# Scatters of the edges' records in small groups beside the nodes' tiles, each group behind one product of its tile

## The chip, the core and the metric

The kernel runs on one core of a Trainium2 chip. A core has TensorE (PE, matrix products; its weight loads are shown as PEld), VectorE (DVE), ScalarE (ACT), GpSimd (POOL) and SyncE (SP), each with a queue of its own that is worked off in order. They signal each other through semaphores. DMA engines move data; here SP and ACT issue the plain transfers, POOL the indirect ones (gathers and scatters by an index list) and some plain ones. The metric is the device time of one execution in microseconds.

## What is computed

A graph layer over 3125 nodes with 512 features and 50000 edges sorted by target node, then a mixture of experts. Cut to what matters:

```python
xn = _layernorm(x)
x = x + gnn(xn, edge_attr_4, edge_attr_32, [src, dst], ...) + mix(xn, ...)   # mix: linear attention over all nodes
x = x + moe(_layernorm(x), ...)

# gnn, for each edge: a gather of both ends' rows, products, and a sum at one end
edge_dst, edge_src = edge_index[0], edge_index[1]
ip1 = einsum('eum,eum->eu', p1[edge_dst], p1[edge_src]) / 3
w = ssp(edge_attr @ W_f1) @ W_f2 * (ssp(s0 @ W_s1) @ W_s2)
out = segment_sum(edge_feat(w, x[edge_src], edge_sh), edge_dst)

# mix: k' and the sums over all nodes first, then every node's query against them
kv = einsum('bshd,bshf->bhdf', k_prime, v)
z = einsum('bshd,bhdf->bshf', q_prime, kv) / (q_prime . k_prime.sum + 1e-6)
```

## The kernel before, in words

The edges are put in order on the chip. There are T = 392 tiles of 128 edges, in 14 chunks of CT = 28 tiles, and NT = 25 tiles of 128 nodes.

*Sort and layer norms.* `records(c)` computes for chunk c, on VectorE, the place of each edge in the sorted list (`places`, into `at_i`) and makes for each edge a record of 48 numbers (its four spherical numbers, both node numbers, the hidden row of its 32 attributes). The chunk's records go to a DRAM tensor `lined` (L262). Between the chunks, the loop at L366 runs `layer_norm(t)` for one or two node tiles: mean and variance, a normalised tile `xn`, four transposes on TensorE (L345), a copy of them by ScalarE into `xT` (L346), the product with the key weights `ps_k` (L349), the feature map (VectorE L303, ScalarE L304, VectorE L305), and two products `ps_kx` (L353) that add this tile to sums over all nodes. So each tile passes from engine to engine some ten times; buffers of two tiles let neighbours overlap.

*Scatters.* POOL takes the records of a chunk back into SBUF (`recall`, L399, two buffers `again`) and scatters them, one indirect DMA of 128 records for each of the 392 edge tiles (L407), to their sorted places in `recs`. It needs a chunk's `lined` and its `at_i`, and nothing else. In the program the loop stands behind all the layer norms; as POOL's queue holds nothing else there, it runs as soon as its data are there.

*Folding, queries, nodes' tiles.* The sums are folded with value and output weights into `kvw` and `norm` (L463 to L500). The queries (L507 on) run over 7 chunks of 512 nodes and 2 groups of heads: products `ps_q`, feature map, one product `ps_nm` (L518) and a division. Then, for each chunk of 512 nodes, the gate network, and for each node tile t the rows that the edges will gather, `rows_d` and `rows_s` (L592, L593), and the node's own part: `ps_own` gets two products of the query (L598) and four of the gated features (L602), and is added to `out` (L606). Four PSUM buffers serve `ps_p1` and `ps_nd`, two serve `ps_own`, so PE can be about two tiles ahead of those who empty them.

*Edge loop.* The first load of sorted records (`fetch`, q = 0) waits for all 392 scatters. Then POOL gathers the two ends' rows for each tile of edges (L658, L662), which also need `rows_d` and `rows_s` complete. The loop over 220 pairs of edge tiles runs in an order written out by hand. The mixture of experts follows.

The order on each engine is made by a scheduler from the order of the program and the dependencies; `tc.issue_after` holds an instruction behind another in that order.

Of the kernel before, what the change touches and what calls it, by code (L numbers as in the profile page):

```python
# [8 lines left out]
F32 = mybir.dt.float32  # L9
# [7 lines left out]
P = 128  # L17
# [4 lines left out]
REC = 48  # L22
USED = 40
CT = 28
# [14 lines left out]
def gnn_mix_moe_kernel(ctx: ExitStack, tc: tile.TileContext, a: dict, out: bass.AP):  # L39
# [5 lines left out]
    nc = tc.nc  # L45
    N = a["x"].shape[0]
    T = a["src_t"].shape[1]
# [36 lines left out]
    lined = dram.tile([T // CT, P, CT, REC], F32, name="lined")  # L84
    recs = dram.tile([NQ * G * P, REC], F32, name="recs")
# [12 lines left out]
    def waits_for(ins, other):  # L98
        tc.add_manual_dep(
            ins.ins, other.ins.name,  # L100
            mybir.DependencyInfo(mybir.DependencyClass.Sync, mybir.DependencyReason.DATA),
            reason="rows at places known on the chip alone",
        )
# [11 lines left out]
    with ExitStack() as c1:  # L115
        srt = c1.enter_context(tc.tile_pool(name="srt", bufs=1))
        chk = c1.enter_context(tc.tile_pool(name="chk", bufs=2))
# [20 lines left out]
        for r in range(4):  # L138
# [10 lines left out]
        cleared = [  # L149
            nc.gpsimd.dma_start(  # L150
                flat[k * P * zw : (k + 1) * P * zw].rearrange("(p f) -> p f", p=P), zero
            )
            for k in range(10)
        ]
# [42 lines left out]
        at_i = srt.tile([P, T], I32, name="at_i")  # L197
# [26 lines left out]
        placed = []  # L224
# [91 lines left out]
        def layer_norm(t):  # L316
            nonlocal fresh
            n = tn(t)
            rows = slice(t * P, t * P + n)
            x = lnp.tile([P, D], F32, name="x")  # L320
            with tc.issue_after(lines[-2].ins):
                nc.sync.dma_start(x[:n], a["x"][rows, :])
            st = lnp.tile([P, 6], F32, name="bn")
            with tc.issue_after(found[-2].ins):
                nc.vector.bn_stats(st[:n], x[:n])
            mv = lnp.tile([P, 2], F32, name="mv")
            nc.vector.bn_aggr(mv[:n], st[:n])

            rs = lnp.tile([P, 1], F32, name="rs")
            nc.scalar.activation(rs[:n], mv[:n, 1:2], AF.Ln, bias=eps[:n])  # L330
            fresh = nc.scalar.activation(rs[:n], rs[:n], AF.Exp, scale=-0.5)
            off = lnp.tile([P, 1], F32, name="off")
            nc.vector.scalar_tensor_tensor(off[:n], mv[:n, 0:1], -1.0, rs[:n], op0=ALU.mult, op1=ALU.mult)
            rs1 = lnp.tile([P, 1], F32, name="rs1")
            nc.vector.tensor_single_scalar(rs1[:n], rs[:n], 1.0, op=ALU.add)
            xn = lnw.tile([P, D], F32, name="xn")
            nc.scalar.activation(xn[:n], x[:n], AF.Identity, scale=rs[:n], bias=off[:n])

            y = lnw.tile([P, D], F32, name="so_far")
            nc.scalar.activation(y[:n], x[:n], AF.Identity, scale=rs1[:n], bias=off[:n])  # L340
            nc.vector.tensor_add(y[:n], y[:n], b_add[:n])
            nc.sync.dma_start(out[rows, :], y[:n])
            ps = psum.tile([P, 4, P], F32, name="ps_t", tag="mm")
            for b in range(4):
                nc.tensor.transpose(ps[:, b, :n], xn[:n, b * P : (b + 1) * P], ident[:n, :n])  # L345
            nc.scalar.copy(xT[:, :, rows], ps[:, :, :n])  # L346
            ps_k = psum.tile([P, NH * FD], F32, name="ps_k", tag="mm")
            for k in range(4):
                nc.tensor.matmul(ps_k[:n], xT[:, k, rows], w_rk[:, k, :], start=(k == 0), stop=(k == 3))  # L349
            kf = lnw.tile([P, NH * FD], F32, name="kf")  # L350
            feature_map(kf[:n], ps_k[:n], n, NH * FD, lnw, NH * FD)
            for g in range(2):
                nc.tensor.matmul(  # L353
                    ps_kx[g], kf[:n, g * P : (g + 1) * P], xn[:n], start=(t == 0), stop=(t == NT - 1)
                )
            nc.vector.tensor_add(kfs[:n], kfs[:n], kf[:n])

        with tc.issue_after(found[0].ins):
            nc.vector.tensor_add(b_add[:, :MUL], b_add[:, :MUL], b_o0)
# [3 lines left out]
        ps_b = psum.tile([P, P], F32, name="ps_bo", tag="mm")  # L363
        nc.tensor.matmul(ps_b, b_row, w_o[0], start=True, stop=True)
        nc.vector.tensor_add(b_add[:, :MUL], b_add[:, :MUL], ps_b)
        for c in range(1, NC):  # L366
            records(c)
            for t in range((c - 1) * NT // (NC - 1), c * NT // (NC - 1)):
                layer_norm(t)
            if c == 3:  # L370
                with tc.issue_after(fresh.ins):
                    w_g1 = load("w_g1", [P, 2, 2 * MUL], a["W_g1"].rearrange("(k p) f -> p k f", p=P))
                    w_g2 = load("w_g2", [P, 2, 2 * MUL], a["W_g2"].rearrange("(k p) f -> p k f", p=P))
                    b_g1 = load("b_g1", [P, 2], a["b_g1"])
                    b_g2 = load("b_g2", [P, 2], a["b_g2"])
                    w_pre0 = load("w_pre0", [P, MUL], a["W_pre0"])
                    b_pre0 = load("b_pre0", [P, 1], a["b_pre0"])
                    w_pre1 = load("w_pre1", [P, MUL], a["W_pre1"])
                    w_nd0 = load("w_nd0", [P, MUL], a["W_nd0"])
                    w_nd1 = load("w_nd1", [P, MUL], a["W_nd1"])  # L380
                    b_nd0 = load("b_nd0", [P, MUL], _rows(a["b_nd0"], P, MUL))
                    w_s1 = load("w_s1", [P, 2, HID], a["W_s1"][0 : 2 * MUL, :].rearrange("(k p) f -> p k f", p=P))
                    w_v = load("w_v", [P, 4, D], a["W_v"].rearrange("(k p) f -> p k f", p=P))
                    w_out = load("w_out", [P, 4, D], a["W_out"].rearrange("(k p) f -> p k f", p=P))
            elif c == 5:
                with tc.issue_after(fresh.ins):
                    w_rq = by_random("W_qT")
# [2 lines left out]
        with tc.issue_after(made.ins):  # L390
            nc.vector.tensor_add(w_s1p, w_s1[:, 0, :], w_s1[:, 1, :])


        again = {}

        def recall(c):
            if c < T // CT:
                again[c] = chk.tile([P, CT, REC], F32, name="again", bufs=2)
                nc.gpsimd.dma_start(again[c], lined[c])  # L399

        recall(0)
        for c in range(T // CT):
            for i in range(CT):
                t = c * CT + i
                if i == CT // 2:
                    recall(c + 1)
                put = nc.gpsimd.indirect_dma_start(  # L407
                    out=recs[:, :], out_offset=bass.IndirectOffsetOnAxis(ap=at_i[:, t : t + 1], axis=0),
                    in_=again[c][:, i, :], in_offset=None,
                )  # L410
                placed.append(put)


        for put in placed:
            for z in cleared:
                waits_for(put, z)
            tc.declare_no_dep(put.ins, group="put", reason="edges have places of their own")
            tc.add_to_no_dep_group("put", put.ins)
        c0.close()
        work = c1.enter_context(tc.tile_pool(name="work1", bufs=2, reuse_waits="tile"))  # L420
        w1p = c1.enter_context(tc.tile_pool(name="w1p", bufs=1, reuse_waits="tile"))
# [7 lines left out]
        for c in range(NCH):  # L429
            m = cn(c)  # L430
            cols = slice(c * CH, c * CH + m)
# [30 lines left out]
        norm = w1p.tile([P, 2, P], F32, name="norm")  # L462
        for g in range(2):  # L463
# [6 lines left out]
            for k in range(4):  # L470
                nc.tensor.matmul(
                    ps, kxT[:, k, g * P : (g + 1) * P], w_v[:, k, g * GH * HD : (g + 1) * GH * HD],
                    start=(k == 0), stop=(k == 3),
# [33 lines left out]
        for c in range(NCH):  # L507
            m = cn(c)
            cols = slice(c * CH, c * CH + m)
            for g in range(2):  # L510
                ps = psum.tile([P, CH], F32, name="ps_q", tag="mm")
                for k in range(4):
                    nc.tensor.matmul(
                        ps[:, :m], w_rq[:, k, g * P : (g + 1) * P], xT[:, k, cols], start=(k == 0), stop=(k == 3)
                    )
                feature_map(qf[:, g, cols], ps[:, :m], P, m, work, CH)
                ps = psum_b.tile([P, CH], F32, name="ps_nm", tag="mb")
                nc.tensor.matmul(ps[:, :m], norm[:, g, :], qf[:, g, cols], start=True, stop=True)  # L518

                rn = work.tile([P, CH], F32, name="rn", tag="one")  # L520
                nc.scalar.activation(rn[:, :m], ps[:, :m], AF.Ln, bias=tiny)
                mapped = nc.scalar.activation(rn[:, :m], rn[:, :m], AF.Exp, scale=-1.0)
                nc.vector.tensor_mul(qf[:, g, cols], qf[:, g, cols], rn[:, :m])
# [16 lines left out]
        for c in range(NCH):  # L540
# [27 lines left out]
            for t in tiles_of(c):  # L568
# [30 lines left out]
                        ps[:n], qf[:, g, t * P : t * P + n], kvw[:, g, :], start=(g == 0), stop=False  # L599
                    )  # L600
                for b in range(4):
                    nc.tensor.matmul(  # L602
                        ps[:n, b * P : (b + 1) * P], xg[:, b, lo : lo + n], w_ndo[0 if b == 0 else 1],
                        start=False, stop=(b == 3),
                    )
                nc.vector.tensor_add(y[:n], y[:n], ps[:n])  # L606
                nc.sync.dma_start(out[rows, :], y[:n])

# [709 lines left out]
```

## Time and profile before

| | |
|---|---|
| median of 3 runs | 3443.95 us (3419.78 to 3478.66) |
| span of the profiled execution | 3436.8 us |
| PE / DVE / ACT / POOL busy | 2690.3 / 1925.0 / 1507.8 / 1802.1 us |
| scatters (L407) | 392, mean 1028 ns, from 70.6 to 681.5 us |
| layer norms of the nodes | to about 608 us |
| first gather of the edge loop | 918 us |

The page cuts the span into 40 slices of 86 us and gives each engine's busy share of a slice as a digit. A row of the timeline has the start and the length in us, the engine, the line, the operation, the tiles written and read, and in brackets how long the engine had been idle before it and what ended that. "remote" there means that no instruction in the trace was found to have released it at that time; "issue" means that nothing was waited for that the profile shows. In a list of waits the numbers are the total in us, the number of times and the longest.

### The profile page before, as it was taken

The numbers are of one execution on the slowest core, as the hardware profiler recorded it, in microseconds if no ns is written. First come the engines' busy times: TensorE is split into PE (matmuls) and PEld (weight loads), VectorE is DVE, ScalarE is ACT, GpSimd is POOL, SyncE is SP. The second block draws the span as 40 slices with busy tenths as digits, with TensorE's granted clock in tenths as the row PEclk, the third lists the DMA queues.
The fourth block names the chain that finished last, engine by engine and source line by source line (L and its number), as shares of the span: only waits on it lengthen the run. The fifth ranks groups of instructions, "written<-read, shape, count | busy, mean of one in ns | idle before, by whom it ended". The sixth has DMA issues, their size and how long they took to land. (4 is left out here: it accounts for less than half of the span.)

```text
span 3436.8 us, 43142 instructions
## 1 busy us (share of the span) xinstructions
PE 2690.3 (78%) x14070; PEld 1744.5 (51%) x14070; DVE 1925.0 (56%) x3979; ACT 1507.8 (44%) x4332; POOL 1802.1 (52%) x1812
## 2 busy tenths in 40 slices
PE   3141315499479999999999999995889888898887
PEld 2131203256334444444444444444777777777776
DVE  5151304332279999999999999986322222221221
ACT  2020203132168888888888888873111111111111
POOL 2747575700266666666666666622444444444443
PEclk7565658799789999999999999997999999999999
DMA  6241313015478888888888888736423424736251
GB/s 236 65 138 50 105 57 113 25 56 200 151 230 255 254 267 253 257 262 254 256 263 255 264 257 253 230 103 211 185 62 106 150 62 172 281 108 244 62 205 34
DMA packets 197209, 600.80 MB, mean 175 GB/s; under 512 B 57286, under 2 KB 82811, under 8 KB 184953
## 3 DMA queue, kind: packets, MB, share of 16 engines
q0 software_dynamic: 140208, 508.84, 45.4%
q1 hardware_dynamic: 50440, 82.93, 7.3%
q10 hardware_dynamic: 6336, 6.28, 0.6%
q8 instruction: 112, 1.84, 0.2%
q14 instruction: 113, 0.92, 0.1%
HBM read 661.63 MB, written 120.32 MB: 228 GB/s over the span
## 5 line engine op out<-in xcount | busy, mean ns | idle before, releaser
L829 PE MATMUL ps_s<-ft,one 128*128 128x512 f32 x1760 | 793.0, 593 | 2.1 <-DVE ft L816 2.0
L658 POOL DMA_INDIRECT gd<-rows_d,rec x440 | 443.4, 1008 | 525.1 <-DMA rec<-recs 236.7
L1210 DVE TENSOR_SCALAR h<-ps_f,bias 128x128 f32<-128x128 f32 x336 | 113.8, 350 | 763.0 <-PE ps_f L1201 417.5
L662 POOL DMA_INDIRECT gx<-rows_s,rec x440 | 451.0, 1025 | 134.1 <-issue 129.2
L1201 PE MATMUL ps_f<-h,we 128*128 128x128 f32 x3584 | 447.7, 288 | 81.4 <-ACT h L1208 81.3
L812 ACT ACTIVATE ft<-ft,rec 128x128 f32<-128x128 f32 x1320 | 410.1, 389 | 201.3 <-DVE ft L805 146.0
L829 PEld LDWEIGHTS ps_s<-ft,one 128*128 128x128 f32 x1760 | 323.5, 194 | 321.6 <-issue 277.2
L1201 PEld LDWEIGHTS ps_f<-h,we 128*128 128x128 f32 x3584 | 434.8, 202 | 93.0 <-ACT h L1208 89.6
L407 POOL DMA_INDIRECT recs<-again,at_i x392 | 403.1, 1028 | 125.9 <-issue 121.6
L1208 ACT ACTIVATE h<-ps_f,bias 128x128 f32<-128x128 f32 x336 | 118.3, 366 | 674.5 <-PE ps_f L1201 406.5
L767 ACT ACTIVATE dot<-gx,rec 128x128 f32<-128x128 f32 x880 | 280.7, 397 | 0.0
L1224 POOL DMA_INDIRECT out<-r,out_at x56 | 57.3, 1022 | 419.3 <-DVE r L1223 385.5
L1149 POOL DMA_INDIRECT we<-w_rows,w_at x224 | 224.4, 1002 | 98.9 <-issue 63.1
L757 DVE TENSOR_TENSOR wt<-wt,wb 128x1024 f32<-128x1024 f32 x220 | 267.0, 1214 | 13.1 <-remote 13.0
L746 PE MATMUL wa<-w_f,hT 32*128 32x512 f32 x880 | 249.9, 644 | 10.5 <-issue 10.5
L750 PE MATMUL wb<-w_s,hT 32*128 32x512 f32 x880 | 249.9, 644 | 6.3 <-DVE wt L757 6.3
L1201 PE MATMUL ps_f<-xt,we 128*128 128x128 f32 x1792 | 219.1, 281 | 32.8 <-ACT xt L1170 25.7
L1201 PEld LDWEIGHTS ps_f<-xt,we 128*128 128x128 f32 x1792 | 209.6, 195 | 47.7 <-ACT xt L1170 34.9
L674 DVE TENSOR_TENSOR prod<-gd,gx 128x768 f32<-128x768 f32 x220 | 209.4, 952 | 37.9 <-issue 20.7
L349 PE MATMUL ps_k<-r_W_kT,xT 128*128 128x256 f32 (+1 forms) x200 | 68.4, 481 | 186.2 <-issue 105.0
L816 DVE TENSOR_TENSOR ft<-gx,wt 128x768 f32<-128x768 f32 x220 | 213.3, 970 | 0.0
L682 PEld LDWEIGHTS ps_ip<-ident,prod 128*128 128x128 f32 x1320 | 145.1, 142 | 125.7 <-issue 125.7
(300 smaller groups left out, 4162.2 us busy)
## 6 DMA issues: line engine op xcount, KB each, us to landing
w_rows<-in_Wh POOLq DMA_DIRECT2D x24, 1024.0 KB
rows_s<-r SPq DMA_DIRECT2D x24, 448.0 KB
recs<-zero POOLq DMA_DIRECT2D x10, 1056.0 KB
rec<-recs SPq DMA_DIRECT2D x110, 96.0 KB
lined<-rec SPq DMA_DIRECT2D x14, 672.0 KB
again<-lined POOLq DMA_DIRECT2D x14, 672.0 KB
w_rows<-in_Wo POOLq DMA_DIRECT2D x8, 1024.0 KB
gd<-rows_d,rec POOLq DMA_INDIRECT x440
```

Of the source, the lines that this page charges most:

```text
L407: put = nc.gpsimd.indirect_dma_start(out=recs[:, :], out_offset=bass.IndirectOffsetOnAxis(ap=at_i[:, t : t + 1], axis=0), in_=again[c][:, ...
L658: nc.gpsimd.indirect_dma_start(out=Q.gd[:, (i + 2) % G, :], out_offset=None, in_=rows_d[:, :], in_offset=bass.IndirectOffsetOnAxis(ap=reci ...
L662: Q.last = nc.gpsimd.indirect_dma_start(out=Q.gx[:, i, :], out_offset=None, in_=rows_s[:, :], in_offset=bass.IndirectOffsetOnAxis(ap=reci[ ...
L746: nc.tensor.matmul(wa[:, k, :], Q.hT[r, 0, :], w_f2[r, :], start=True, stop=True)
L750: nc.tensor.matmul(wb[:, k, :], Q.hT[r, 1, :], w_s2[r, :], start=True, stop=True)
L757: nc.vector.tensor_mul(R.wt, R.wt, wb)
L767: nc.scalar.activation(R.dot[:, c - 1, k, :], x[:, i, c * MUL : (c + 1) * MUL], AF.Copy, scale=Q.rec[:, i, c : c + 1])
L812: nc.scalar.activation(R.ft[:, k, D + c * MUL : D + (c + 1) * MUL], R.ft[:, k, 2 * D :], AF.Copy, scale=Q.rec[:, i, c : c + 1],)
L816: nc.vector.tensor_mul(R.ft[:, :, MUL:D].rearrange("p k (b u) -> p k b u", b=3), x[:, :, MUL:].rearrange("p k (b u) -> p k b u", b=3), w3. ...
L829: nc.tensor.matmul(R.ps, R.one[:, k, :], R.ft[:, k, m * D : (m + 1) * D], start=(k == 0 and m == 0), stop=(k == 1 and m == 1),)
L1149: nc.gpsimd.indirect_dma_start(out=dst, out_offset=None, in_=src, in_offset=bass.IndirectOffsetOnAxis(ap=at[:, j : j + 1], axis=0), bounds ...
L1201: nc.tensor.matmul(pss[f], ws[l][:, k, f * P : (f + 1) * P], h[:, k, :], start=(k == 0), stop=(k == 3))
```

## The change

The scatters are no longer one loop behind the layer norms. A function `place(upto, behind)` issues all scatters that are due up to a given time, counting 1.3 us for each, and lets the first one of the group wait for an instruction of PE. It is called beside each layer norm, each query step and each node tile, with due times that rise by 8 us, 5 us and 7 us a call. `layer_norm` hands back its last product for this. The aim, by the reason written into the wait, is that POOL gives way to PE: scatters are to run in small groups through the whole of the nodes' work.

```diff
@@ layer_norm
             for g in range(2):
-                nc.tensor.matmul(
+                last = nc.tensor.matmul(
                     ps_kx[g], kf[:n, g * P : (g + 1) * P], xn[:n], start=(t == 0), stop=(t == NT - 1)
                 )
             nc.vector.tensor_add(kfs[:n], kfs[:n], kf[:n])
+            return last
@@ before the loop of records and layer norms
+        again = {}
+
+        def recall(c):
+            if c < T // CT:
+                again[c] = chk.tile([P, CT, REC], F32, name="again", bufs=2)
+                nc.gpsimd.dma_start(again[c], lined[c])
+
+        def place(upto, behind=None):
+
+            for t in range(len(placed), min(T, max(0, int(upto / 1.3)))):
+                c, i = divmod(t, CT)
+                if t == 0:
+                    recall(0)
+                if i == CT // 2:
+                    recall(c + 1)
+                put = nc.gpsimd.indirect_dma_start(
+                    out=recs[:, :], out_offset=bass.IndirectOffsetOnAxis(ap=at_i[:, t : t + 1], axis=0),
+                    in_=again[c][:, i, :], in_offset=None,
+                )
+                if behind is not None:
+                    tc.add_manual_dep(
+                        put.ins, behind.ins.name,
+                        mybir.DependencyInfo(mybir.DependencyClass.Sync, mybir.DependencyReason.DATA),
+                        reason="POOL gives way to PE",
+                    )
+                    behind = None
+                placed.append(put)
+
         for c in range(1, NC):
             records(c)
             for t in range((c - 1) * NT // (NC - 1), c * NT // (NC - 1)):
-                layer_norm(t)
+                place(8 * t + 42)
+                place(8 * t + 50, layer_norm(t))
@@ behind the layer norms: recall(0), the loop over all scatters and their dependencies
-        recall(0)
-        for c in range(T // CT):
-            for i in range(CT):
-                t = c * CT + i
...
@@ queries
-                nc.tensor.matmul(ps[:, :m], norm[:, g, :], qf[:, g, cols], start=True, stop=True)
+                last = nc.tensor.matmul(ps[:, :m], norm[:, g, :], qf[:, g, cols], start=True, stop=True)
+                place(275 + 5 * (2 * c + g), last)
@@ nodes' tiles
                 for b in range(4):
-                    nc.tensor.matmul(
+                    last = nc.tensor.matmul(
                         ps[:n, b * P : (b + 1) * P], xg[:, b, lo : lo + n], w_ndo[0 if b == 0 else 1],
                         start=False, stop=(b == 3),
                     )
+                place(355 + 7 * t, last)
                 nc.vector.tensor_add(y[:n], y[:n], ps[:n])
                 nc.sync.dma_start(out[rows, :], y[:n])
@@ behind the nodes' tiles
+        place(2 * T)
+
+        for put in placed:
+            for z in cleared:
+                waits_for(put, z)
+            tc.declare_no_dep(put.ins, group="put", reason="edges have places of their own")
+            tc.add_to_no_dep_group("put", put.ins)
```

The scheduler moves the scatters of a group that wait for nothing ahead of the one that waits. In the built program of the changed kernel the waits therefore stand before scatter 33, 39, 45, 51, 57, 65, ... with 1 to 21 scatters from one to the next.

More of the change, by code (lines that the diff above doesn't have):

```diff
@@ L391, in gnn_mix_moe_kernel @@
             nc.vector.tensor_add(w_s1p, w_s1[:, 0, :], w_s1[:, 1, :])
[L394 to L399, printed above, removed]
-        recall(0)
-        for c in range(T // CT):
-            for i in range(CT):
-                t = c * CT + i
[L405 to L418, printed above, removed]
         c0.close()
```

## The prediction

> **What bounds the kernel now.** I read the slices of the page first, then busy time by stage, then the waits of the first 700 us, then single rows of the timeline. The slices (86 us each) show where the engines idle: TensorE is nearly idle for eight slices, and POOL works just there.
>
> ```profile
> PE   3141315499479999999999999995889888898887
> POOL 2747575700266666666666666622444444444443
> ```
>
> The first eight slices belong to the sort and the nodes' layer norms. Cut by stage (layer norms; folding of the attention weights; queries; nodes' tiles; ramp of the edge loop; edge loop):
>
> ```profile
> 70.00:608.00 538.00, 173.78 (x585) 112.35 (x586) 158.45 (x511) 105.22 (x218) 349.95 (x356) 0.65 0.27 88
> 608.00:650.00 42.00, 19.30 (x50) 10.12 (x49) 29.03 (x46) 4.76 (x11) 35.30 (x24) 0.64 0.10 30
> 650.00:730.00 80.00, 58.40 (x138) 26.13 (x138) 23.61 (x38) 22.55 (x36) 24.84 (x26) 0.87 0.03 9
> 730.00:917.00 187.00, 162.61 (x831) 108.65 (x829) 57.60 (x90) 42.85 (x81) 0.00 (x0) 0.94 0.42 153
> 917.00:984.00 67.00, 25.31 (x97) 15.93 (x97) 18.19 (x31) 14.55 (x44) 41.84 (x42) 0.56 0.71 217
> 984.00:2260.00 1276.00, 1243.24 (x5656) 630.23 (x5654) 1260.92 (x2305) 1080.74 (x3352) 876.75 (x870) 1.00 0.81 255
> ```
>
> Columns: stretch, length, busy PE, weight load, DVE, ACT, POOL, clock, DMA share, GB/s. The layer norms last 538 us, yet no compute engine has more than 174 us of work in them. Only POOL is busy, with 345 of the 392 scatters; the DMA engines are at 0.27. In the nodes' tiles it is the reverse: PE 163 of 187 us, POOL nothing. So two pieces of work that could lie side by side lie end to end. What do the idle engines wait for?
>
> ```profile
> DVE fm L303 <- remote: 151.1, 10, 28.9
> ACT xT L346 <- remote: 104.5, 9, 26.8
> ACT xn L337 <- remote: 59.6, 4, 25.4
> PE ps_k L349 <- ACT xT L346: 81.1, 8, 45.0
> ```
>
> Both L303 and L346 only read what TensorE has just written, yet they wait 10 to 29 us each time, and the releaser is "remote", that is, nothing that the rows show. One such pair:
>
> ```profile
> 175.72 1.12 PE L345 MATMUL ps_t<-ident,xn 128*128 128x128 f32 x4 [35.60 <-ACT rs L330]
> 196.92 0.59 ACT L346 COPY xT<-ps_t 128x512 f32<-128x512 f32 x1 [20.45 <-remote]
> ```
>
> The transposes end at 176.84; ScalarE starts its copy of them at 196.92, having been idle. In the trace's record of PE's semaphore the update itself is late: it follows its product by 0.01 us when POOL is quiet (215 to 240 us), by 2 to 4 us some ten scatters into a burst (82 to 95, 242 to 256), by 20 to 25 us deep in one (110 and 177). Scatters come as bursts of 86 to 101 back to back (70.6 to 199.4 is the first). So a long burst delays the signals between the other engines, and that, not work, sets the 538 us. Between bursts (528 to 560) the products of L353 that end a tile come every 5 to 8 us.
>
> The scatters end long before anyone wants them:
>
> ```profile
> 681.51 0.95 POOL L407 DMA_INDIRECT recs<-again,at_i  x1 [0.30 <-issue]
> 917.97 0.99 POOL L658 DMA_INDIRECT gd<-rows_d,rec  x1 [235.51 <-DMA rec<-recs]
> ```
>
> POOL then idles 235.5 us until the nodes' rows are stored. The path to the edge loop is therefore: layer norms, folding, queries, nodes' tiles, first gather at 918. What the change makes of that time is what it gains; the 2520 us after it hold the same instructions in the same order.
>
> **What the Trainium skill says.** "Perfetto Trace Analysis", section "Tensor Engine Instruction (MATMUL, LD_WEIGHTS)": the propagation of the semaphore lies behind the end that the profiler reports, so it is in no row. The trace agrees and gives it sizes, 0.01 to 25 us. "SBUF — State Buffer", section "Who interferes with whom": only DVE and GpSimd share a port pair, and PE and ACT wait on nobody. By it ScalarE's 20.45 us above can't be a port, and the trace has no other engine holding one. "Trainium Architecture — The Big Picture", section "What this means for kernel authors": engines are independent unless a semaphore lies between them. Here the semaphores themselves are slowed by POOL; no page prices that, so I size it from the trace alone.
>
> **The change, part by part.** *Emission.* The loop of scatters behind the layer norms goes; the same 392 scatters and 14 reloads come out of `place`. The built program has the same order on PE, DVE, ACT and SP; on POOL only the points of the reloads shift by a few scatters. No instruction is added but waits.
>
> *Waits.* 63 scatters now wait for a product: 25 for a tile's second L353, 14 for a query step, 24 for a node tile. Between two waits stand 1 to 12 scatters, three times 19 to 21. One scatter with its gap is 128.8 us / 100, or 1.26 us where DVE is quiet. Behind a waiting scatter on POOL stand all later scatters, reloads and the edge loop's gathers; for them waits only the first load of records (all 392). It had 235 us of slack; now the last scatter waits for the last full node tile, so its landing lies beside the stores of the last rows, which took from 909 to 918 before. I take nothing for it; at worst some 5 us.
>
> *What the layer norms become.* The first 32 scatters are unpaced, as now, up to 111 us, so tile 1 ends at 109 as now. Then 23 tiles. POOL's share: scatters 33 to 201 over 24 tiles is 7.0 each, times 1.26 = 8.8 us, with a reload (0.6 us) every fourth tile 9.0. DVE's own work is 158/25 = 6.3 us a tile. POOL's pace is the larger, and PE's signals come a little late inside each group: I take 10 us. 109 + 23 × 10 = 339, and 6 for the tail: 345. Low: 9.1 each, 320. High: 13 each (each tile pays a further 3 to 4 us, the delay found ten scatters into a burst), 410.
>
> *Folding.* 42 us now, with one wait of 14 us; 19 scatters (24 us) run into it. 40; between 30 and 55.
>
> *Queries.* Undisturbed a step is 4.3 us (L518 at 700, 704, 709), 14 steps 60 us. POOL has 57 scatters there, 72 us, and two or three reloads. 90, between 75 and 120.
>
> *Nodes' tiles to the first gather.* 187 us now with POOL silent. 115 scatters, 145 us, now lie beside them; two tiles of PSUM buffers absorb signals that are a few us late. I take 15% more: 215, between 187 and 260.
>
> Sum: 345 + 40 + 90 + 215 = 690 against 918, so 228 us less: 3444 − 228 = 3216. The low ends give 612 (3138), the high ends 845 (3371). No choice goes far below: POOL's 392 × 1.26 + 14 × 0.6 = 502 us from 70.6 end at 573, and the gathers queue behind.
>
> **Rivals.** *A: signals freeze for the whole of a group.* Then group and work add: layer norms 6.3 + 9.0 = 15.3 a tile, 109 + 23 × 15.3 = 461; folding 42; queries 60 + 72 + 24 = 156; nodes 187 + 145 = 332. Gather at 991, 73 us later: 3517, slower. For it: the 20 to 25 us. Against: tile 0 ran through the first 12 us of the first burst, and in the edge loop POOL issues gathers of the same kind in groups of eight with 2 us pauses (877 us busy of 1276) while PE is busy 97%. I give it 4%. *B: the lateness isn't POOL's doing* (it comes with the sort's DVE work or with a DMA). Then the layer norms stay, the waits stretch POOL to the nodes' end, and the gather comes at 918 to 925: 3444 to 3451. For it: at 201 to 209.5 and from 347 to 355 signals were still late with POOL stopped. Against: DVE was idle in those waits, and before 700 us every stretch in which all three engines idle for over 10 us lies in a burst or within 21 us of its end. 7%. *C: pacing helps by half*, since the late signals outlast a group by up to 8 us, as at 201: 17 us a tile, 109 + 23 × 17 = 500, then 50, 110, 235: gather at 895, 3421, within 2%; with half of that, 13 a tile, it is the high end above. 9% for the bad half. *D: groups small enough that signals hardly lag*: 3138, inside my case.
>
> **How the numbers follow.** The forecast's case (gather at 612 to 845) has 80%; 3216 is its likeliest. A, B and C share 20%, all above, so 3135 to 3375 leaves about 2 in 10 out; the top is the high sum, the bottom the low one. Of the 80% nearly all is faster by over 2% (69 us); with a part of C, faster 0.88. B and the bad half of C: same 0.08. A: slower 0.04.
>
> **What would show it.** Right: the layer norms end near 345; "remote" waits at L303 and L346 fall from 29 and 27 us to under 8; scatters spread to the end of the nodes' tiles; POOL's wait before the first gather falls from 235 to about 10 us; the edge loop is unchanged. Wrong: waits of 20 us remain between groups (C), L353 comes every 15 us or more (A), or the nodes' tiles take over 260 us.

## The result, and the profile after

The changed kernel takes 3282.57 us (3274.78 to 3285.96, four runs) where the kernel before takes 3431.86 us (3416.68 to 3478.66, four runs): a ratio of 0.958, interval 0.952 to 0.963. It is faster, by 149 us. The forecast was 3216, 67 us lower, with 3135 to 3375 as its range.

One thing has to be known before any later number is read. The experiments were run on five chips, with the kernel before beside them on each. It takes 3009 to 3020 us on four of them and 3512 us on the third. So there are two conditions, called *prompt* and *late* below, by what TensorE's semaphore does in them. The result above and the trace of before belong to the late one. A kernel is compared with the kernel before on the same chip. On the third chip six of the seven runs of the kernel before are slow ones, above 3507 us, and one is at 3437.62, so no interval can be given there.

The slices of the page, now 82 us each, in the order of the two lines shown of before:

```profile
PE   3455584783999999999999999975988888888887
POOL 2775766435666666666666666413444444444443
```

TensorE's near-idle start has shrunk: the row of nines begins at slice 11 instead of 13, and slices 4 to 7, which read 1 3 1 5, read 5 5 8 4. By stage (layer norms, queries, nodes' tiles to the first gather, edge loop; columns as before):

```profile
70.00:362.00 292.00, 166.91 (x587) 110.94 (x588) 158.71 (x512) 104.72 (x218) 204.12 (x193) 0.74 0.41 135
...
405.00:475.00 70.00, 60.13 (x144) 26.72 (x142) 23.84 (x39) 23.40 (x39) 45.60 (x46) 0.93 0.11 35
475.00:767.00 292.00, 185.68 (x825) 119.92 (x824) 57.40 (x89) 41.26 (x80) 139.81 (x147) 0.78 0.36 120
...
824.00:2105.00 1281.00, 1246.09 (x5663) 632.50 (x5664) 1264.12 (x2305) 1083.86 (x3358) 877.50 (x868) 1.00 0.80 254
```

The layer norms fell from 538 to 292 us with the same work on PE and DVE. The nodes' tiles rose from 187 to 292 us. The edge loop is as it was (1276 to 1281). So 246 us were won in one stage and 10 in the queries, and 105 us of them given back in the nodes' tiles. The waits of the layer norms and queries, 60 to 475 us:

```profile
DVE fm L303 <- remote: 69.4, 7, 17.4
...
ACT xT L346 <- remote: 17.9, 3, 9.8
```

L303 waited 151.1 us for "remote" before, L346 104.5 us; 69.4 and 17.9 us are left. POOL was seldom held for this: of the 25 scatters that wait for a tile's product, it stood still before seven, 23.5 us in all. At the others the product was done when POOL came to them. In the nodes' tiles, which before had no scatters beside them, such waits are new:

```profile
ACT r L589 <- remote: 57.3, 4, 30.3
...
DVE y L614 <- remote: 34.4, 5, 15.1
```

One more such wait, in a run of 26 scatters (515 to 548 us): the products end at 529.29, and ScalarE, idle, reads them from 551.96 on.

```profile
528.27 1.02 PE L554 MATMUL ps_g<-n,w_g 128*128 128x512 f32 x2
...
551.96 1.27 ACT L556 ACTIVATE hT<-ps_g,b_g 128x512 f32<-128x512 f32 x2 [20.91 <-remote]
```

TensorE itself falters there. These rows of the timeline lie in a run of 31 scatters and one reload without a pause (471 to 511 us). TensorE stands idle 1 to 3 us before each single product of one tile's eight, and the bracket names no releaser but "issue":

```profile
501.37 0.37 PE L592 MATMUL ps_nd<-w_nd,xg 128*128 128x128 f32 x1 [3.00 <-issue]
502.77 0.37 PE L592 MATMUL ps_nd<-w_nd,xg 128*128 128x128 f32 x1 [1.03 <-issue]
```

Outside the runs the eight take 1.06 us in one row. From tile 0's to tile 23's sum y (L614) is 232 us (506 to 738); before, with POOL silent, it was 140 (749 to 889). Where the scatters stand singly, one a tile (702 to 738), the tiles come as fast as before: eight sums in 36 us (before 39).

The end of the stage:

```profile
738.40 0.96 POOL L384 DMA_INDIRECT recs<-again,at_i  x1 [3.44 <-PE ps_own L609]
...
747.89 10.72 DVE L647 MEMSET acc<- 128x12800 f32 x1 [3.26 <-issue]
758.54 0.62 DVE L614 TENSOR_TENSOR y<-y,ps_own 53x512 f32<-53x512 f32 x1
759.18 0.24 SPq L615 DMA_DIRECT2D out<-y  x1
...
767.24 0.99 POOL L673 DMA_INDIRECT gd<-rows_d,rec  x1 [27.88 <-DMA rec<-recs]
```

POOL's 235.5 us before the first gather are 27.9. What stands in them is a chain: the clearing of acc on VectorE (10.7 us; acc lies where the records' buffers were, so it comes behind the last scatter), the last tile's y queued behind it, that tile's store on SyncE, and the loads of the sorted records queued behind that store.

Last, the semaphores. The trace records when PE's semaphore is updated. For each update I take the time since the last product that updates this semaphore had ended; the update was late by that much or more. The table has the longest of each stage. In the late condition the record holds only 1925 of the changed kernel's 2366 updates, in the prompt one 2340. The very end of the program is left out.

| POOL's work | condition | late by at least |
|---|---|---|
| before, run of 98 scatters (70 to 199 us) | late | 46.0 us |
| after, layer norms (runs of 61, 38, 30, 26 and shorter) | late | 16.5 us |
| after, nodes' tiles, runs of 24 to 31 (480 to 720 us) | late | 22.7 us |
| after, single scatters, most 4.4 us apart (720 to 780 us) | late | 0.01 us |
| before, nodes' tiles, POOL silent (720 to 900 us) | late | 0.01 us |
| edge loop, groups of eight gathers, before and after | late | 3.9 and 1.4 us |
| changed kernel on another chip, all of the run | prompt | 0.12 us |

Of the three compute engines beside POOL only TensorE's updates are late. By the same reading no update of ScalarE is over 0.01 us late in any of these traces, and of VectorE's only one is over 0.04 us (1.66 us). And since the trace models the ends of products, it can't tell a signal that travels slowly from a product that ends late. That single products falter, as above, speaks for TensorE itself being held up, at least in part.

### The profile page after: what moved, and what is told of

Same layout as the page of the kernel before. It is cut to its first block, busy times and chain, and to the rows that moved or that the text cites. A ratio compares the mean times of both kernels' runs of the same rounds, so it can differ in the third digit from the quotient of the medians.

```text
span 3279.7 us, 43207 instructions
## 1 busy us (share of the span) xinstructions
PE 2707.7 (83%) x14070; PEld 1753.0 (53%) x14070; DVE 1926.4 (59%) x3979; ACT 1508.7 (46%) x4332; POOL 1819.0 (55%) x1812
## 5 line engine op out<-in xcount | busy, mean ns | idle before, releaser
L384 POOL DMA_INDIRECT recs<-again,at_i x392 | 415.3, 1060 | 237.1 <-issue 113.8
L697 PE MATMUL ps_ip<-ident,prod 128*128 128x128 f32 x1320 | 172.8, 282 | 43.0 <-DVE prod L689 43.0
```

The source lines that it names most:

```text
L384: put = nc.gpsimd.indirect_dma_start(out=recs[:, :], out_offset=bass.IndirectOffsetOnAxis(ap=at_i[:, t : t + 1], axis=0), in_=again[c][:, ...
L697: nc.tensor.matmul(ps[:, i, :], Q.prod[:, i, b * P : (b + 1) * P], ident, is_transpose=True, start=(b == 0), stop=(b == 2),)
```

## The experiments

The theory: long runs of scatters delay TensorE's signals, the waits break the runs, and what the changed kernel lacks is lost in the runs that remain. Rivals: the place in the program does it, not the waits; or the waits stretch POOL's queue; or the end of the stage lacks it.

### First chip: waits taken out, waits for all, waits for VectorE, few scatters

No waits:

```diff
-                if behind is not None:
+                if False and behind is not None:
```

> The changed kernel with the scatters issued at the same places in the program, but none of them waiting for a product. Theory (long runs of scatters slow the other engines, and only the waits break the runs): POOL has nothing else in its queue there, so it runs ahead as before; layer norms end at 580 to 620 us, first gather at about 918, total 3410 to 3450, as before the change. Rival (the place of the scatters in the program is what helps): total stays near 3283.

All scatters of a group wait:

```diff
-                    behind = None
```

> The changed kernel with every scatter of a group waiting for the group's product, so that the scheduler cannot move the others ahead: 4 to 7 scatters between one product and the next (one group of 25, one of 12), where the changed kernel has 1 to 21. Theory (the runs of 24 to 32 scatters that come of moving ahead cost the nodes' tiles): nodes' tiles to first gather fall from 292 to 215 to 240 us, layer norms stay near 292, total 3210 to 3235. Rival (the number of scatters beside the stage costs, not how they are grouped): 280 to 300 us for the stage, total 3270 to 3295.

The group waits for the VectorE instruction behind the product (here the nodes' tiles; likewise L356 and the division of the queries):

```diff
+                last = nc.vector.tensor_add(y[:n], y[:n], ps[:n])
                 place(355 + 7 * t, last)
-                nc.vector.tensor_add(y[:n], y[:n], ps[:n])
```

> The changed kernel with the first scatter of each group waiting for the VectorE instruction that follows the product (the sum of k', the division of the queries, the addition to out) in place of the product of TensorE. Theory (any pause breaks a run): total within 1% of 3283, 3250 to 3316; the waits come some 2 us later, so it may gain a few us. Rival (the hand-over from TensorE itself matters): layer norms go back towards 538 us, total 3350 or more.

One scatter of each chunk is left:

```diff
+                if i != 0:
+                    placed.append(None)
+                    continue
```

> The changed kernel with only the first scatter of each chunk of 28, 14 in all: it leaves out 378 scatters, so the sorted records are mostly zeros and every edge points to node 0. Only the time up to the first gather is read. Theory (POOL's runs cause the late signals): layer norms end at 220 to 260 us, folding 30, queries 60 to 65, nodes' tiles about 187, first gather at 500 to 550. Rival (the lateness comes with the sort's or the layer norms' own work): waits of 10 to 30 us at L303 and L346 stay, layer norms end at 350 us or later.

Measured, with the kernel before at 3011.02 us: no waits 3010.18 (ratio 0.9997, 0.998 to 1.0014), all wait 3015.49 (1.0015, 1.0002 to 1.0029), wait for VectorE 3060.04 (1.0155, 1.0131 to 1.018), few scatters 2906.35 in one run. Not one of the differences that the theory expected is there, because what it explains isn't: this chip was in the prompt condition. The kernel without waits sends its 392 scatters in one run of 540 us, and its layer norms end at about 262 us, those with 14 scatters at 257. So 378 scatters beside them cost 5 us here. Where they do cost is behind the nodes: with 14 the first gather is at 537 us, with 392 at 634, since POOL is still scattering.

One thing the kernel without waits settles in any condition. In its trace every engine runs the same operations in the same order as in the kernel before (but for two or three pairs of neighbours that start within 0.4 us of each other), POOL with all of its 1812, and with the same number of semaphore waits. So the new place in the program, by itself, changes nothing that an engine sees. What the changed kernel has beyond the kernel before is 63 waits on POOL, and reloads of records at other places in POOL's queue.

The pair of rows that the prediction showed with 20.45 us between, in the kernel without waits on the second chip (same code, same condition):

```profile
174.25 0.60 PE L345 MATMUL ps_t<-ident,xn 128*128 128x128 f32 x4
...
174.89 0.59 ACT L346 COPY xT<-ps_t 128x512 f32<-128x512 f32 x1 [1.35 <-PE ps_t L345]
```

The copy starts 0.04 us behind the transposes, 100 us into the run of scatters, and "remote" stands in no line of that kernel's waits.

### Second chip: the changed kernel itself, and the clearing of acc

The changed kernel unaltered, the two of the first chip again (no waits, all wait), and this:

```diff
-                nc.vector.tensor_add(y[:n], y[:n], ps[:n])
+                added = nc.vector.tensor_add(y[:n], y[:n], ps[:n])
...
-        nc.vector.memset(acc, 0.0)
+        with tc.issue_after(added.ins):
+            nc.vector.memset(acc, 0.0)
```

> The changed kernel, unaltered, beside the kernel before on whatever chip this call gets. If the kernel before takes about 3430 us here (signals of the other engines late inside long runs of scatters), this one takes 3270 to 3300. If it takes about 3010 (signals prompt), there is nothing to gain: 3010 to 3060, and the groups' waits can only stretch the queue of POOL, so the first gather starts later than in the kernel before.

> The changed kernel's places in the program for the scatters, with no group waiting for a product. Theory (the waits break the run, the place does nothing): where the kernel before takes about 3430, this takes 3410 to 3450, scatters in one unbroken run. Rival (the place is enough): 3270 to 3300 as with the waits. Where the kernel before takes about 3010, both say within 0.5% of it.

> Every scatter of a group waits for the group's product, so that the runs are short (4 to 7 scatters) in the nodes' tiles too. Theory (the runs of 24 to 32 scatters between the nodes' tiles cost the changed kernel its missing gain): where the kernel before takes about 3430, this takes 3210 to 3250, 30 to 70 us less than the changed kernel. Rival (the time is the last group's landing and the sort's place, not the runs): 3265 to 3300. Where the kernel before takes about 3010, both say 3010 to 3030.

> The changed kernel with the clearing of acc issued on VectorE behind the last tile's sum y instead of ahead of it. Theory (the clearing of 10.7 us stands between the last scatter and the last store of y, and the records' loads queue behind that store): the first gather starts 10 to 15 us sooner and the kernel is 10 to 15 us faster than the changed kernel. Rival (the clearing is beside the last group's landing, or comes back before the edges' first accumulation): no difference over 4 us.

Measured, prompt condition again, the kernel before at 3019.19 us:

| kernel | us | ratio to before | last scatter | first gather |
|---|---|---|---|---|
| changed kernel | 3070.85 | 1.0183 (1.015 to 1.0217) | 664 | 689 |
| no waits | 3020.11 | 1.0004 (0.9993 to 1.0015) | 608 | 632 |
| all wait | 3022.22 | 1.0008 (0.9996 to 1.002) | 612 | 637 |
| acc cleared later | 3053.27 | 1.0115 (1.008 to 1.0151) | 666 | 672 |

Here the changed kernel is *slower* than before by 1.8%, 11 us more than expected at the worst. Its nodes' tiles as a stage:

```profile
365.00:520.00 155.00, 152.25 (x784) 102.56 (x782) 43.73 (x78) 37.01 (x69) 100.03 (x106) 0.99 0.63 212
```

PE is busy 152 of 155 us with 100 us of scatters beside it; tile 0 to tile 23 takes 140 us (378 to 518), as with POOL silent. The same program took 232 us in the late condition. TensorE is done by 520 and POOL is what the edge loop waits for. POOL's waits from 70 to 666 us:

```profile
POOL recs L384 <- issue: 116.0, 362, 3.2
POOL recs L384 <- DMA again<-lined: 17.8, 5, 7.4
POOL again L374 <- DMA recs<-again,at_i: 12.2, 5, 4.6
POOL again L374 <- issue: 8.0, 5, 2.3
...
POOL recs L384 <- PE ps_own L609: 0.9, 3, 0.3
```

The products, for which the groups wait, cost POOL nothing (0.9 us); the gap of 0.3 us behind each scatter is most of the first line. The rest is at the reloads of records. One of them:

```profile
575.39 0.96 POOL L384 DMA_INDIRECT recs<-again,at_i  x1 [0.30 <-issue]
577.83 0.58 POOL L374 DMA_DIRECT2D again<-lined  x1 [1.48 <-DMA recs<-again,at_i]
582.71 0.98 POOL L384 DMA_INDIRECT recs<-again,at_i  x1 [4.30 <-DMA again<-lined]
```

This reload is queued behind 331 scatters: POOL waits for the last landing from its buffer (1.48 us), and the very next scatter needs what it fetches and waits for that too (4.30). In the code a reload stands 14 scatters ahead of its chunk; in POOL's order scatters have been moved ahead of it. Counted over all gaps above 0.45 us on POOL, less 0.3 each, the changed kernel has 64.3 us from 60 to 670 us and the kernel without waits 14.7. The 49.6 us between them answer to the 50.7 us between their times. In the kernel in which all scatters wait, the same reload is queued behind 310, and no gap exceeds 0.8 us behind the first scatter: with *more* waits it is 49 us faster than the changed kernel. So in the prompt condition waiting as such is harmless, and the reloads' place in the queue is what costs. The kernel that waits for VectorE, on the first chip, belongs here too: it has the same gaps (65.1 us) and nearly the same ratio.

Clearing acc later gives 17.6 us between the medians of four runs each, a little over the 10 to 15 expected. The runs that were traced can't show this total, as they are the fastest of the one kernel and the slowest of the other (3062.78 and 3062.25 us); the order of the work they can show. The end of the scatters in the changed kernel and, below it, in this one:

```profile
664.37 0.96 POOL L384 DMA_INDIRECT recs<-again,at_i  x1 [0.30 <-issue]
...
669.72 10.72 DVE L647 MEMSET acc<- 128x12800 f32 x1 [145.61 <-issue]
680.36 0.62 DVE L614 TENSOR_TENSOR y<-y,ps_own 53x512 f32<-53x512 f32 x1
...
689.07 0.99 POOL L673 DMA_INDIRECT gd<-rows_d,rec  x1 [23.74 <-DMA rec<-recs]
```

```profile
666.47 0.96 POOL L384 DMA_INDIRECT recs<-again,at_i  x1 [0.30 <-issue]
...
671.46 10.72 DVE L648 MEMSET acc<- 128x12800 f32 x1 [148.91 <-issue]
671.67 0.99 POOL L674 DMA_INDIRECT gd<-rows_d,rec  x1 [4.24 <-DMA rec<-recs]
```

In the changed kernel VectorE stood at the clearing for 145.6 us with the last tile's sum behind it; with the later clearing that sum comes at 522 us, and the gather starts 5 us behind the last scatter instead of 25. The clearing itself is hidden beside the first gathers.

### Third chip: reloads in their old place

```diff
+                if i == CT // 2 and c + 1 < T // CT:
+                    loaded.append(recall(c + 1))
+                with tc.issue_after(loaded[-1].ins):
+                    put = nc.gpsimd.indirect_dma_start(
```

> The changed kernel, with every scatter kept behind the newest reload of records, so that a reload is queued on POOL 14 to 18 scatters ahead of the chunk's first scatter, as in the kernel before, instead of 3 to 5. The groups wait for the same products. Theory (where signals are prompt, the changed kernel is slower because its reloads come late: 49.6 us of gaps on POOL, all at a reload): the gaps go, the first gather is back at 630 to 645 from 689, and the kernel takes 0.998 to 1.006 of the kernel before. Rival (the waits for products stretch POOL's queue): 1.012 to 1.02, as the changed kernel. If instead the kernel before takes about 3430 us on this call, with late signals: 3250 to 3285, since there the reloads' gaps also break the runs of scatters.

Measured: 3292.11 us (3285.62 to 3304.43), the kernel before 3511.52 (3437.62 to 3521.11): the late condition, so the expectation's last sentence applies, and it was missed by 7 us. Against the one low run of the kernel before (3437.62) the ratio is 0.958, the changed kernel's own; a single run is weak ground for it. The first gather is at 768, as with the changed kernel (767). Its nodes' tiles over the same stretch, and what they and POOL wait for there:

```profile
475.00:767.00 292.00, 186.42 (x830) 123.52 (x830) 58.81 (x94) 42.65 (x82) 127.35 (x134) 0.79 0.35 118
```

```profile
POOL recs L385 <- PE ps_own L610: 80.6, 15, 11.7
ACT r L590 <- remote: 34.4, 2, 23.1
```

Here POOL isn't the bound: it waits 80.6 us for products. The reloads' gaps that cost 50 us in one condition cost nothing in the other. The theory that those gaps are the loss under prompt signals was not tried by this edit, since the chip was in the other condition; it rests on the sum of gaps and on the kernel with all waits. This run also repeats, on a second chip in the late condition, a gain over the kernel before. And as each reload here stands within three scatters of where the kernel before has it, it is the waits that bring this gain.

### Fourth and fifth chip: both improvements, no waits, and a late start of the waits

All scatters of a group wait and acc is cleared later (both diffs above); no waits, once more; and the first of these without waits beside the first ten tiles:

```diff
-                place(8 * t + 50, layer_norm(t))
+                done = layer_norm(t)
+                place(8 * t + 50, None if t < 10 else done)
```

> Every scatter of a group waits for the group's product (runs of 4 to 7 scatters in the nodes' tiles too), and acc is cleared behind the last tile's sum y. Where the kernel before takes 3430 us or more (late signals): theory (the runs of 24 to 32 scatters between the nodes' tiles and the 28 us behind the last scatter are what the changed kernel lacks) 3190 to 3230, first gather at 680 to 720; rival (the nodes' tiles are slow for another reason, or POOL ends later still as it now waits at each tile) 3265 to 3310, first gather at 755 to 790. Where it takes about 3010 to 3020 (prompt signals): 10 to 17 us under the kernel with all waits alone, so 0.994 to 0.999 of the kernel before.

> The changed kernel's places in the program with no group waiting for a product. Where the kernel before takes 3430 us or more: theory (the waits break the run of scatters, and that is the gain) 3410 to 3520, no gain over the kernel before, with the layer norms ending near 600; rival (the place alone brings the gain) 3270 to 3310. Where it takes about 3010 to 3020: within 0.3% of it by both.

> As the kernel in which every scatter of a group waits and acc is cleared late, but without any wait beside the first ten tiles of the layer norms: 94 scatters go in one run from about 70 to 190 us, after that 4 to 7 at a time. Read by stages. Where the kernel before takes 3430 us or more: theory (only the waits protect the other engines) by 190 us no more than 3 or 4 tiles of the layer norms are done, as in the kernel before (3, the fourth at 215), against 8 in the changed kernel; after the run they go at 10 us a tile or less, and the nodes' tiles with their short runs take 200 to 240 us to the first gather instead of 292; in all 3220 to 3290. Rival (the place in the program protects them): 7 or 8 tiles by 190 us, and 3200 to 3250. Rival for the nodes' tiles (their length has another cause than the runs): 280 us or more again. Where the kernel before takes about 3010 to 3020: 2990 to 3005, and nothing is told apart.

Both chips were in the prompt condition, so the expectations for the late one stay untested. All wait and acc later: 2995.87 us against 3009.20 (0.995, 0.9935 to 0.9966), first gather at 617 us:

```profile
612.28 0.96 POOL L384 DMA_INDIRECT recs<-again,at_i  x1 [0.30 <-issue]
...
617.27 10.72 DVE L647 MEMSET acc<- 128x12800 f32 x1 [99.70 <-issue]
617.45 0.99 POOL L673 DMA_INDIRECT gd<-rows_d,rec  x1 [4.21 <-DMA rec<-recs]
```

The scatters run without a gap and the gathers follow them in 5 us. No waits: 3007.72 (0.9989, 0.9974 to 1.0005). Waits from the tenth tile on: 2998.35 against 3019.84 (0.9936, 0.9911 to 0.9961), which tells nothing apart, as expected. Under prompt signals the first and the last of these beat the kernel before by half a per cent and the changed kernel, measured on another chip, by over two. Under late signals neither was run.

## Why the prediction was right, and where not

*What bounds the kernel: right where it was read.* In the late condition a long run of scatters holds up TensorE's products and signals, and through them the others. The strongest evidence is one program in both conditions: the changed kernel's tiles 0 to 23 take 232 us and 140 us with the same scatters beside them, and 140 us with POOL silent in the late condition. The layer norms show the same, when the end of each tile's products L353 is compared between the two conditions. In the run of 38 scatters the changed kernel under late signals falls 31 us behind itself under prompt ones (tile 2). It stays 30 to 36 us behind up to tile 10, at 210 us, beside groups of 12, 6 and 8 and the first half of the run of 61. Behind that run, at tile 12, it is 69 us behind, and 97 at the end. It was not a matter of the place in the program, as the kernel without waits is on every engine the kernel before; so the waits brought the gain. A run without waits beside the changed kernel under late signals is still lacking: this kernel met prompt signals three times. That the forecast was tried in the late condition, in which its trace was taken, was luck: on the second chip the same change came out 1.8% slower.

Some readings of the trace were too narrow. "Signals between the other engines" are TensorE's alone. The bursts "of 86 to 101" count reloads and pass over one: they are 98, 84, 84, 28 and 98 scatters. L303 and L346 waited 1.8 to 28.9 us for "remote", not 10 to 29 each time, and besides the two updates that were 20 to 25 us late one is 46.0 us late (157 us). The low and high sums of the layer norms lack the 6 us of tail (324 and 414 for 320 and 410).

*Layer norms: right in size, less so in the working.* 345 us predicted (320 to 410), 362 measured; 11.0 us a tile from the second on ((362 − 109) / 23) for 10 taken. But the even pace of 7 scatters a tile didn't come about. Only seven of the 25 waits held POOL, and runs of 61 and 26 scatters remained; in the later half of the run of 61 two tiles took over 26 us each. That such a stage averaged near 10 us a tile is partly luck. *Folding:* 43 for 40. *Queries:* 70 for 90, under the low end of 75: POOL did 45.6 us of work in them instead of the 72 reckoned, as its queue was behind.

*Nodes' tiles: the step that failed.* 215 us was forecast, with 260 as the high end; 292 was measured. "I take 15% more" is the mis-sized term: it came to 56%. The working had seen that three groups hold 19 to 21 scatters, but priced the stage as if its groups were the usual small ones. It also reckoned with 115 scatters, and as POOL's queue was behind, 142 fell into the stage. Of the 24 waits 14 held POOL, eight of them at the single scatters at the end; at the other ten the product was done when POOL reached them. So runs of 31, 26, 24, 26 and 24 scatters formed, and PE's signals came 22.7 us late, or more, at the worst place in them. The two tiles of PSUM buffers could not absorb waits of 15 to 30 us. Whether the length of the runs or the number of scatters is what costs here stays open: the kernel in which all wait was not run under late signals. Rival A's rule for this stage (work and scatters add, 332) was nearer than the forecast's.

*The last scatter.* "At worst some 5 us" was right, although POOL waited 27.9 us before the first gather instead of about 10. From tile 23's sum to the gather it is 29 us in both kernels (738 to 767, 889 to 918); the clearing of acc was in the old 187 us already. Under prompt signals the same chain costs, since there the scatters end last.

*The sum.* First gather at 767 for 690, 77 us late. From there to the end it is 2515 us (3282.6 − 767.2), for 2526 in the forecast (3444 − 918). 77 less 11 is the 67 us of the miss. The 11 us are no gain: the kernel before had a median of 3443.95 us when the forecast was made and 3431.86 with the fourth run, which leaves 2514 behind its first gather.

*The rivals.* A fell in the layer norms (11.0 us a tile for 15.3). B, that lateness isn't POOL's doing, fell too: the gather came at 767, not 918. C fell (895). Of the signs set down as proving the forecast wrong, two came true in the nodes' tiles: waits of over 20 us, and more than 260 us. The chance of slower, 4%, was given to A alone. No rival held what four of the five chips showed: signals that are prompt, so that nothing is to be won in the layer norms. The changed kernel was run on one of these, and lost 1.8%.

*What stays open:* what makes a chip, or an hour on it, late or prompt; whether TensorE's products end late or only its signals do; and whether groups of 4 to 7 throughout shorten the nodes' tiles in the late condition.

## What to carry to other kernels

A wait bounds a run only where it still holds when the queue reaches it; after a scheduler has moved instructions, read the runs from the trace, not from the code. When work is emitted in pieces so that it can be hoisted, check what it overtakes: here the reloads that feed it, 50 us once POOL was the bound. And before tuning against late signals, see whether another chip has them: the sign of the result turned with it. Clearing acc behind the last tile's sum helped under prompt signals (17.6 us); it would remove a chain that the late condition shows as well, but was not run there by itself or with the waits.

## What was not expected of the hardware

The kernel before takes 3009 to 3020 us on four chips of the experiments, 3512 us on the third, and 3432 us beside the changed kernel. The operations themselves are hardly slower: a scatter occupies POOL for 0.96 us in both, and the edge loop is no longer (from its first to its last product of the sums over edges, ps_s, 1333 us in the kernel before under late signals and 1334 without waits under prompt ones). Nor is a slower DMA the reason: the median packet takes 159 ns on POOL's queue and 84 ns on the first of the plain ones in both conditions. The difference lies in the nodes' stages and the mixture of experts, where POOL gathers weights (989 us from the first of these gathers to the last under late signals, 867 under prompt ones); there too ScalarE and VectorE wait for "remote" in the late condition only, VectorE's L1210 for 301.4 us in the kernel before. In the late condition PE's updates follow its products by 0.01 us whenever POOL is silent or sends one scatter every 4.4 us, at worst by 3.9 us or more in the edge loop's groups of eight gathers, and at worst by 16 to 46 us or more in stages with runs of 24 to 98 scatters, while VectorE's and ScalarE's updates are not late. Under prompt signals no update of PE is over 0.12 us late beside a run of 392.
